# Batch 0's keys by block products, begun ahead of m, and a new order of the first loads

## The chip, the cores and the metric

The kernel runs on one core of one Trainium2 chip. The metric is the time of one execution on the device, in microseconds (us). Each version is run several times, and the median is compared. The engines are TensorE (PE), VectorE (DVE), ScalarE (ACT), GpSimd (POOL) and SyncE (SP, which issues most of the transfers).

## The reference

For each of 16 batches there are 100 tokens `x` of width 640 and 722 context rows of width 384, of which the last four (`ca`) are treated apart. All numbers are float32.

```python
query = hidden_states @ Wq
keyt = enc @ Wk                # enc: the first 718 context rows
valt = enc @ Wv
hs = _mha(query, keyt, valt)   # 8 heads of 80
ca_q1 = jnp.einsum('btc,th->bch', ca, Wq_ca)[:, indices, :]
ca_hs1 = _mha(ca_q1, residual, residual)
ca_hs2 = _mha(ca_hs1 @ Wq, ca @ Wk_ca, ca @ Wv_ca)
out = (hs + ca_hs2) @ Wout + b_out + residual
```

## The kernel before

**Tiling.** The context's 718 rows are cut into three thirds of 239 or 240 (`KT` = 240), each of which is two halves of up to `KN` = 120; the width 384 is three chunks of 128 (`CC` = 3), and 640 is five (`HC` = 5). The list `KC` numbers the six halves. `enc` holds the context of one batch, transposed, seven of its nine chunk-by-third pieces in one tile and two in a tile called `rest`.

**Two ways to the keys and values.** The plain way multiplies each third by each chunk of weights: `first_keys` with `chunk_keys` does so for batch 0's keys (line 565), nine products of 128x240 for each of five output chunks, and `first_values` for its values (line 381). The other way is a scheme of 15 block products in place of 18, in the manner of fast matrix multiplication: `enc_sums` (line 506, 13 additions on GpSimd) and `weight_sums` (line 528, 12 subtractions on VectorE) make sums of pieces; the classes `Values` and `Keys` then run products of these sums in the order of `V_PLAN` and `K_PLAN`. A block of keys is two matmuls of 128x240 (line 471). The first result for a place is copied there by ScalarE (line 413), and each later one is added by VectorE (line 411). The blocks use PSUM banks named A to E: `Keys.open` takes A and B from the pool psk, C to E from the pool ps1. `last_keys` does the fifth output chunk the plain way. From batch 1 on, keys and values come by blocks; the weight sums for that were made in the prologue.

**The second attention.** `m` (line 1036) is Wq transposed times the keys of the last four tokens for all batches, k2 (line 1013, masked by five VectorE multiplications at line 1025 into `k2T`). VectorE copies each chunk of m (line 1044), `keys()` spreads one batch's part of it into `m2` on GpSimd (line 718), and `Second.products` multiplies it by x (line 746). `scores1` is GpSimd work on what came out (lines 781 and 788), followed by a softmax.

**PSUM.** There are three pools of two slots: psk and ps1 of one bank, ps2 of two banks (`pair`, or `bank` for the first half of a pair). `psum()` takes turns between psk and ps1 by a counter, `turn`.

```python
    def psum(name):

        turn[0] += 1
        return (psumk if turn[0] % 2 else psum1)(name)
```

**Order of the work.** There are two regimes. The prologue, up to line 1123, is ordered by the planner of the framework, which may bring ready work forward on each engine; only loads marked `in_order` keep their order among themselves, and blocks under `tc.issue_after` stay behind a named instruction. From `tc.manual_schedule` (entered just before the loop over the 16 batches) each of the five engines runs its instructions in the order of the code. The prologue is, in the code's order: loads; five idle matmuls (line 1001); the first values for four of the six halves; k2 and m; the second attention's first steps for batch 0; 15 transposes of Wk (line 1059, copied into `wk_sb` at line 1062); 15 copies that lay Wq out as `wq_sb` (lines 1070 and 1077); the weight sums for Wk; batch 0's keys; the four tokens' values (line 1090); and the queries for batches 0 and 1 (line 541). The loop's first step then makes scores (line 620), in two slots of ps2 for the first and third pair of halves. The remaining two halves of batch 0's values are made in the loop.

**Loads.** The transfers issued by SP and ScalarE share eight completion semaphores in turn, and the instruction that issues a transfer waits until the one eight places earlier has landed. Wk, transposed, is loaded in nine pieces (`load_packed`, eight of them of 32 partitions) into the tile that later holds the keys; Wq transposed is loaded into the tile that later holds Wout.

Of the kernel before, what the change touches and what calls it, by code (L numbers as in the profile page):

```python
# [10 lines left out]
ALU = mybir.AluOpType  # L11
# [4 lines left out]
NH, D = 8, 80  # L16
# [116 lines left out]
def kernel(  # L133
# [134 lines left out]
    )  # L268
    enc = enc_tile("enc_0"), rest_tile("rest_0")

    def load_first(lo, hi, u, cols):

        for c in range(lo, hi):
            k = u * (KT - 1)
            in_order(
                nc.sync.dma_start(
                    out=a_raw(enc, u, c)[:, cols],
                    in_=enct[0][:, c, k + cols.start : k + cols.stop],
                )
            )  # L280

    load_first(0, CC, 1, slice(0, KN))
    for g in range(2):
        for c in range(CC):
            nc.scalar.dma_start(
                out=wv_sb[:, 2 * c + g],
                in_=wv[c * P : (c + 1) * P, g * (H // 2) : (g + 1) * (H // 2)],
            )
    load_first(0, CC, 1, slice(KN, KT))
    load_first(0, CC, 2, slice(0, KT))  # L290
    tokens = vb_tile("tokens")
    cat_sb = tokens[:, CC, : CC * B * T].rearrange("p (c n) -> p c n", c=CC)
    wkca_sb = tokens[:, :CC, :]
    in_order(nc.sync.dma_start(out=cat_sb, in_=cat.rearrange("p c b t -> p c (b t)")))
    in_order(nc.sync.dma_start(out=wkca_sb, in_=wkca.rearrange("(c p) n -> p c n", p=P)))
    wqt_sb = wout_sb
    wkt_sb = kT.rearrange("p c u k -> p c (u k)")
    in_order(nc.sync.dma_start(out=wqt_sb, in_=wqt.rearrange("(c p) r -> p c r", p=P)))
    load_first(0, CC, 0, slice(0, KT))
    xT = inp.tile([P, 2, HC, S], F32, tag="xT", name="xT_0")  # L300
    in_order(nc.sync.dma_start(out=xT, in_=xt[0:2].rearrange("b p c s -> p b c s")))
    ca_0 = small.tile([S, T, S], F32, tag="ca", name="ca_0", bufs=2)
    in_order(nc.sync.dma_start(out=ca_0, in_=cas[0].unsqueeze(0).to_broadcast([S, T, S])))
    load_packed(
        lambda **ends: in_order(nc.sync.dma_start(**ends)), wkt_sb[:, :, :CAD], wkt
    )
    halves = [t[:, u] for t in [scores_tile(f"wq_{i}") for i in range(NP)] for u in range(2)]
    room = halves.pop()
    wq_in = [t[:, :H] for t in halves]
# [224 lines left out]
            for tag, n in (("qp", 2), ("qz", 1))  # L534
        ]

    def queries(p, xT, tiles, n):
        qp, qz = tiles
        q_ps = psum(f"q_ps_{p}_{n}")
        for c in range(HC):  # L540
            nc.tensor.matmul(  # L541
                q_ps[:, : 2 * S].rearrange("p (j s) -> p j s", j=2),
                wq_sb[:, c, n * P : (n + 1) * P],
                xT[:, :, c, :],
                start=(c == 0),
                stop=(c == HC - 1),
            )
        if n < 4:
            nc.scalar.copy(qp[:, n // 2, n % 2], q_ps[:, : 2 * S])
        else:  # L550

            for u in range(2):
                nc.scalar.mul(
                    qz[:, 0, :, u * S : (u + 1) * S],
                    q_ps[:, : 2 * S].rearrange("p (j s) -> p j s", j=2),
                    qmask[:, u : u + 1],
                )


    def chunk_keys(n, banks, weights, enc):  # L560
# [18 lines left out]
                )  # L579
            )  # L580
        return copies

    def first_keys(enc):
        for n in range(HC - 1):
            banks = [psum(f"kT_ps_0_{n}_{k}") for k in range(2)]
            weights = [wk_sb[:, 2 * c + n % 2, n // 2] for c in range(CC)]
            chunk_keys(n, banks, weights, enc)
        last_keys(0, enc)

    def last_keys(b, enc):  # L590
        banks = pair(f"kT_ps_{b}")
# [409 lines left out]
        nc.tensor.matmul(idle_ps[:, :P], idle, idle, start=True, stop=True)  # L1001


    for i in (1, 4, 2, 5):
        first_values(i, enc, (act, act))
    weight_sums(nc.vector, wv_sb, there=wv_there)


    k2_ps = psum("k2_ps")
# [11 lines left out]
    for n, heads in enumerate(HEADS):  # L1021
        cols = len(heads) * B * T
        k2T.append(room[:, at : at + cols])
        at += cols
        nc.vector.tensor_tensor(
            k2T[n].rearrange("p (h k) -> p h k", h=len(heads)),
            k2_ps[:, n * B * T : (n + 1) * B * T]
            .unsqueeze(1)
            .to_broadcast([P, len(heads), B * T]),
            hmask[:, n, : len(heads)].unsqueeze(2).to_broadcast([P, len(heads), B * T]),  # L1030
            ALU.mult,
        )
    for c in range(HC):
        m_ps = psum(f"m_ps_{c}")
        for n, heads in enumerate(HEADS):
            nc.tensor.matmul(
                m_ps[:, heads[0] * B * T : (heads[-1] + 1) * B * T],
                wqt_sb[:, n, c * P : (c + 1) * P],
                k2T[n],
                start=(n == 0),  # L1040
                stop=(n == HC - 1),
                skip_group_check=True,
            )
        copied = nc.vector.tensor_copy(
            m_sb[c].rearrange("p (b h t) -> p h b t", h=NH, t=T),
            m_ps.rearrange("p (h b t) -> p h b t", h=NH, b=B),
        )
        nc.sync.dma_start(out=m_d[c], in_=m_sb[c])
    second = Second(0, xT, ca_0)
    keys(load_m(0))  # L1050
    summed = second.products()
    second.copy()
    second.scores1()
    keys(load_m(1))

    for c in range(HC):
        w_ps = psum(f"w_ps_{c}")
        for cc in range(CC):
            nc.tensor.transpose(
                w_ps[:, cc * P : (cc + 1) * P], wkt_sb[:, c, cc * P : (cc + 1) * P], ident  # L1060
            )
        act(
            wk_sb[:, c % 2 : 6 : 2, c // 2] if c < HC - 1 else wk4,
            w_ps[:, : CC * P].rearrange("p (a n) -> p a n", a=CC),
        )

    with tc.issue_after(summed.ins):
        for c in range(HC):
            for u in range(2):
                nc.vector.tensor_copy(  # L1070
                    wq_sb[:, c, 2 * u * P : 2 * (u + 1) * P].rearrange(
                        "p (a r k) -> p a r k", a=2, r=RG
                    ),
                    wq_in[c].rearrange("p (r k) -> p r k", r=RG)[:, :, u * D : u * D + 64]
                    .rearrange("p r (a k) -> p a r k", a=2),
                )
            nc.vector.tensor_copy(
                wq_sb[:, c, 4 * P :].rearrange("p (h k) -> p h k", h=NH),
                wq_in[c].rearrange("p (h k) -> p h k", h=NH)[:, :, 64:],
            )  # L1080
    with tc.issue_after(summed.ins):
        weight_sums(nc.vector, wk_sb, False)
    first_keys(enc)
    weight_sums(nc.vector, wk_sb, True)

    va = wide("va")[:, : H // 2]
    va_ps = psum("va_ps")
    for c in range(CC):
        for n in range(2):
            nc.tensor.matmul(  # L1090
# [8 lines left out]
    for n in range(2):  # L1099
# [1 line left out]
            out=va_d[:, n * (H // 2) : (n + 1) * (H // 2)],  # L1101
            in_=va[n * B * T : (n + 1) * B * T],
        )
    with tc.issue_after(copied.ins):
        nc.vector.tensor_reduce(
            qmask, ident.rearrange("p (r u k) -> p u r k", r=RG, u=2), AX.XY, ALU.add
        )
    tiles = queries_tiles(0)
    for n in range(HC):
        queries(0, xT, tiles, n)  # L1110

    xT_at = [None]
    last, enc_next, second_next = None, load_rest(1, load_enc(1)), Second(1, xT)
    engines = {
        mybir.EngineType.Pool,
        mybir.EngineType.PE,
        mybir.EngineType.DVE,
        mybir.EngineType.Activation,
        mybir.EngineType.SP,
    }  # L1120
    ctx.enter_context(tc.manual_schedule(engines=engines))
    for b in range(B):
        p = b // 2
        e_in, now = enc, second
# [271 lines left out]
```

## Time and profile before

| what | value |
|---|---|
| median of 3 runs | 944.52 us (944.06 to 944.62) |
| the profiled execution: its time, its span | 944.18 us, 942.5 us |
| granted clock of TensorE, mean | 1.0 |
| busy: PE, DVE, ACT, POOL | 934.5, 675.5, 364.6, 623.1 us |
| chain that ended last, share of PE | 94% |
| values of batch 0, four halves: first product to end | 3.66 to 18.28 us |
| keys of batch 0 on PE | 30.94 to 49.33 us |
| first scores on PE | 59.68 us |

Times in the profile count from the span's start. Busy times overlap, so they do not add up to the span. A row of the order in time gives start, duration, engine, line, operation, output and inputs, the shape, how many instructions are merged in it, and in brackets how long the engine was idle before it and what ended that. One float32 product shows as two matmul records.

### The profile page before, as it was taken

How to read it: one execution, taken by the hardware profiler on the slowest of the kernel's cores; microseconds unless marked ns; L12 is line 12 of the kernel's file. 1: busy time of each engine (PE TensorE's matmuls, PEld its weight loads, DVE VectorE, ACT ScalarE, POOL GpSimd, SP SyncE). 2: the span in 40 equal slices, each digit the busy share in tenths (PEclk: the TensorE clock that was granted, in tenths of full speed). 3: DMA queues.
4: the chain of work that ended last, by engine and by line, in shares of the span. 5: the costliest groups of instructions: out<-in, count | busy, mean ns of one | idle time of the engine just before them, and what ended most of it. 6: DMA issues, size and time to landing. Idle time of an engine off the chain costs nothing.

```text
span 942.5 us, 25630 instructions
## 1 busy us (share of the span) xinstructions
PE 934.5 (99%) x11215; PEld 796.0 (84%) x11215; DVE 675.5 (72%) x1084; ACT 364.6 (39%) x605; POOL 623.1 (66%) x565
## 2 busy tenths in 40 slices
PE   9999999999999999999999999999999999999998
PEld 6998879788797888988789887987989888897866
DVE  3559794977929788595955959578693886949684
ACT  1244443424334244433424334244431534334241
POOL 5857966776738767595863948757694576848514
PEclk9999999999999999999999999999999999999999
DMA  8822024040310404004050120403113030110300
GB/s 263 297 64 84 3 70 127 1 130 3 94 60 1 117 2 130 10 9 123 1 151 3 35 83 1 139 1 95 38 40 113 1 112 7 54 58 1 95 8 29
DMA packets 45367, 62.48 MB, mean 66 GB/s; under 512 B 13448, under 2 KB 37320, under 8 KB 43656
## 3 DMA queue, kind: packets, MB, share of 16 engines
q1 hardware_dynamic: 41720, 42.97, 15.1%
q0 software_dynamic: 2512, 16.72, 6.0%
q8 instruction: 88, 1.44, 0.7%
q10 hardware_dynamic: 1024, 1.15, 0.4%
q14 instruction: 23, 0.19, 0.1%
HBM read 55.26 MB, written 5.57 MB: 65 GB/s over the span
## 4 chain that ended last, share of the span: by engine, by line
PE 94%; DVE 3%; issue 1%; DMA 0%; ACT 0%; POOL 0%; ACTq 0%; DVEq 0%
PE s_ps L620 12%; PE a_ps L1317 12%; PE v_psA L440 10%; PE v_psB L440 8%; PE kT_ps L565 8%; PE q_ps L541 7%; PE k_psA L471 7%; PE o_ps L951 7%; PE k_psB L471 6%; PE v_psC L440 3%; PE k_psC L471 3%; PE y_ps L746 2%; PE v_psD L440 2%; PE v_psE L440 2%; PE v_ps L381 1%; PE k_psE L471 1%
## 5 line engine op out<-in xcount | busy, mean ns | idle before, releaser
L781 POOL TENSOR_TENSOR e<-ca,g 100x800 f32<-100x800 f32 x64 | 99.3, 1563 | 142.5 <-DVE most L1156 127.5
L870 POOL TENSOR_TENSOR hs<-vb,p 100x640 f32<-100x640 f32 x64 | 105.6, 1659 | 46.1 <-DVE p L856 32.3
L877 POOL TENSOR_TENSOR hs<-hs,hs 100x640 f32<-100x640 f32 x48 | 113.9, 2372 | 3.8
L1317 PEld LDWEIGHTS a_ps<-vs,st 120*36 120x36 f32 (+3 forms) x3072 | 109.1, 125 | 5.6 <-issue 5.5
L1317 PE MATMUL a_ps<-vs,st 120*36 120x81 f32 (+3 forms) x3072 | 111.9, 233 | 0.0
L506 POOL TENSOR_TENSOR enc<-enc 128x240 f32<-128x240 f32 x135 | 98.8, 741 | 16.7 <-DMA enc<-in_enct 9.6
L440 PE MATMUL v_psA<-wv_sb,enc 128*120 128x320 f32 x352 | 109.7, 434 | 0.0
L1144 DVE TENSOR_TENSOR st<-st,over 120x1600 f32<-120x1600 f32 x48 | 107.5, 2242 | 0.0
L637 ACT COPY st<-s_ps 120x800 f32<-120x800 f32 x64 | 49.7, 829 | 135.6 <-PE s_ps L620 135.6
L620 PE MATMUL s_ps<-qp,kT 32*120 32x100 f32 x3072 | 97.6, 263 | 0.0
L620 PEld LDWEIGHTS s_ps<-qp,kT 32*120 32x120 f32 x3072 | 94.8, 179 | 1.6 <-issue 0.2
L788 POOL TENSOR_TENSOR e<-e,e 100x800 f32<-100x800 f32 x48 | 90.4, 1884 | 3.8
L440 PE MATMUL v_psB<-wv_sb,enc 128*120 128x320 f32 x296 | 91.8, 433 | 0.0
L471 PE MATMUL k_psA<-enc,wk_sb 128*128 128x240 f32 x360 | 87.7, 366 | 0.2 <-DVE kT L411 0.2
L1329 DVE RECIPROCAL rs<-a_ps 100x4 f32<-100x4 f32 x32 | 5.8, 183 | 111.0 <-PE a_ps L1317 111.0
L471 PEld LDWEIGHTS k_psA<-enc,wk_sb 128*128 128x128 f32 x360 | 68.2, 190 | 17.3 <-POOL e L788 0.7
L440 PEld LDWEIGHTS v_psA<-wv_sb,enc 128*120 128x120 f32 x352 | 63.0, 183 | 22.9 <-DVE vs L411 0.8
L1152 ACT ACTIVATE st<-st 120x1600 f32<-120x1600 f32 x48 | 73.9, 1539 | 21.8 <-DVE st L1144 21.7
L1156 DVE TENSOR_TENSOR most<-most,st 120x800 f32<-120x800 f32 x64 | 65.8, 1029 | 22.9 <-ACT st L631 21.8
L471 PE MATMUL k_psB<-enc,wk_sb 128*128 128x240 f32 x300 | 73.1, 366 | 0.0
L440 PEld LDWEIGHTS v_psB<-wv_sb,enc 128*120 128x120 f32 x296 | 54.1, 183 | 21.9 <-DVE vs L411 0.4
L541 PE MATMUL q_ps<-xT,wq_sb 128*128 128x200 f32 x400 | 69.1, 333 | 0.0
(146 smaller groups left out, 1734.1 us busy)
## 6 DMA issues: line engine op xcount, KB each, us to landing
vb<-va_d POOLq DMA_DIRECT2D x16, 1000.0 KB, 7.6
enc<-in_enct SPq DMA_DIRECT2D x30, 240.0 KB, 3.8
enc<-in_enct SPq DMA_DIRECT2D x15, 360.0 KB, 3.5
xT<-in_xt SPq DMA_DIRECT2D x8, 500.0 KB, 4.7
rest<-in_enct SPq DMA_DIRECT2D x31, 120.0 KB, 6.6
xn<-in_x SPq DMA_DIRECT2D x11, 320.0 KB, 4.1
out<-xn SPq DMA_DIRECT2D x11, 320.0 KB, 2.8
ca<-in_cas SPq DMA_DIRECT2D x16, 156.2 KB
```

Of the source, the lines that this page charges most:

```text
L440: nc.tensor.matmul(at[0][j][:KN, : H // 2], a_form(self.enc, f)[:, j * KN : (j + 1) * KN], wv_there.get(f, wv_sb[:, W_AT[f]]), start=first ...
L471: nc.tensor.matmul(at[:, i * KT : (i + 1) * KT], wk_sb[:, W_AT[f], i], a_form(self.enc, f), start=(first and i == 0), stop=last, skip_grou ...
L506: nc.gpsimd.tensor_tensor(out, left, right, op)
L541: nc.tensor.matmul(q_ps[:, : 2 * S].rearrange("p (j s) -> p j s", j=2), wq_sb[:, c, n * P : (n + 1) * P], xT[:, :, c, :], start=(c == 0), ...
L565: nc.tensor.matmul(bank[:, i * KT : (i + 1) * KT], weights[c], a_raw(enc, u, c), start=(i == 0 and c == 0), stop=(c == CC - 1), skip_group ...
L620: nc.tensor.matmul(s_ps[r][:n, 256 * a + lo : 256 * a + hi], kT[rows, c, u, j * KN : (j + 1) * KN], rhs, start=(a == 0 and c == 0), stop=( ...
L781: first = nc.gpsimd.tensor_tensor(to, self.ca[:, t, :].unsqueeze(1).to_broadcast([S, NH, S]), g[:, :, t].unsqueeze(2).to_broadcast([S, NH, ...
L788: nc.gpsimd.tensor_tensor(e, e, to, ALU.add)
L870: first = nc.gpsimd.tensor_tensor(to, vb[:S, t, :].rearrange("p (h d) -> p h d", h=NH), p2[:, :, t].unsqueeze(2).to_broadcast([S, NH, D]), ...
L877: nc.gpsimd.tensor_tensor(sums, sums, to, ALU.add)
L1144: return nc.vector.tensor_tensor(st[i], st[i], top.over[:KN].unsqueeze(1).to_broadcast([KN, 2, ROWS]), ALU.subtract,)
L1317: nc.tensor.matmul(a_v[lo:hi, h % 4], st[i // 2][: KEYS[i], i % 2, h * S + lo : h * S + hi], block(i, h // 4)[: KEYS[i], h % 4], start=(i ...
```

## The change

**Loads.** The first loads of the context's thirds take two chunks in one transfer where they lie side by side: two transfers for three. The first half of Wv's columns still comes in three transfers, the second half in one. The remaining third of the context is loaded right behind the other two, then Wk, then the four tokens with their key weights, and Wq transposed; x and `ca` come after that.

**Order by hand from the first values on.** `tc.manual_schedule` is entered before the first values instead of before the loop, so each engine runs the whole prologue in the code's order, which is rewritten: the first values, `enc_sums` for batch 0, the sums of Wv, the transposes of Wk, the sums of Wk, k2, five key blocks, m, the copies of Wq, two blocks, the second attention's first steps, the four tokens' values, and the queries with two blocks after each of the first four and `last_keys` before the fifth.

**Keys.** `first_keys` is gone; batch 0's keys are `Keys(0, enc)` and `last_keys(0, enc)`.

**Banks.** m takes its banks from ps1 alone; the four tokens' values and the queries of batches 0 and 1 take theirs from ps2 (`bank`).

```diff
+        k = u * (KT - 1)
+        for to, lo, hi in (
+            ((enc[0][:, :3], 0, 3),),
+            ((enc[1][:, :1], 0, 1), (enc[0][:, 3:5], 1, 3)),
+            ((enc[0][:, 5:7], 0, 2), (enc[1][:, 1:], 2, 3)),
+        )[u]:
             in_order(
                 nc.sync.dma_start(
...
-    load_first(0, CC, 1, slice(0, KN))
-    for g in range(2):
-        for c in range(CC):
+    load_first(1, slice(0, KN))
+    for g, parts in ((0, [slice(c, c + 1) for c in range(CC)]), (1, [slice(0, CC)])):
+        for c in parts:
             nc.scalar.dma_start(
...
-    load_first(0, CC, 1, slice(KN, KT))
-    load_first(0, CC, 2, slice(0, KT))
+    load_first(1, slice(KN, KT))
+    load_first(2, slice(0, KT))
+    load_first(0, slice(0, KT))
+    wkt_sb = kT.rearrange("p c u k -> p c (u k)")
+    load_packed(
+        lambda **ends: in_order(nc.sync.dma_start(**ends)), wkt_sb[:, :, :CAD], wkt
+    )
...
-    load_first(0, CC, 0, slice(0, KT))
...
-    load_packed(
-        lambda **ends: in_order(nc.sync.dma_start(**ends)), wkt_sb[:, :, :CAD], wkt
-    )
...
-    def queries(p, xT, tiles, n):
+    def queries(p, xT, tiles, n, get=psum):
         qp, qz = tiles
-        q_ps = psum(f"q_ps_{p}_{n}")
+        q_ps = get(f"q_ps_{p}_{n}")
...
+    ctx.enter_context(tc.manual_schedule(engines=engines))
     for i in (1, 4, 2, 5):
         first_values(i, enc, (act, act))
+    enc_sums(enc)
     weight_sums(nc.vector, wv_sb, there=wv_there)
+
+    for c in range(HC):
+        w_ps = psum(f"w_ps_{c}")
+        for cc in range(CC):
+            nc.tensor.transpose(
+                w_ps[:, cc * P : (cc + 1) * P], wkt_sb[:, c, cc * P : (cc + 1) * P], ident
+            )
+        act(
+            wk_sb[:, c % 2 : 6 : 2, c // 2] if c < HC - 1 else wk4,
+            w_ps[:, : CC * P].rearrange("p (a n) -> p a n", a=CC),
+        )
+    weight_sums(nc.vector, wk_sb)
...
+    k0 = Keys(0, enc)
+    k0.go(3)
+    k0.go(2)
     for c in range(HC):
-        m_ps = psum(f"m_ps_{c}")
+        m_ps = psum1(f"m_ps_{c}")
...
     keys(load_m(0))
-    summed = second.products()
+
+    for c in range(HC):
+        for u in range(2):
+            nc.vector.tensor_copy(
+                wq_sb[:, c, 2 * u * P : 2 * (u + 1) * P].rearrange(
...
+    k0.go(2)
+    second.products()
     second.copy()
     second.scores1()
     keys(load_m(1))
...
-    first_keys(enc)
-    weight_sums(nc.vector, wk_sb, True)
+    nc.vector.tensor_reduce(
+        qmask, ident.rearrange("p (r u k) -> p u r k", r=RG, u=2), AX.XY, ALU.add
+    )
 
     va = wide("va")[:, : H // 2]
-    va_ps = psum("va_ps")
+    va_ps = bank("va_ps")
...
+    xT_at = [None]
+    last, enc_next, second_next = None, load_rest(1, load_enc(1)), Second(1, xT)
     tiles = queries_tiles(0)
     for n in range(HC):
-        queries(0, xT, tiles, n)
...
+        queries(0, xT, tiles, n, bank)
+        k0.go(2)
+        if n == HC - 2:
+            last_keys(0, enc)
```

## The prediction

> **What bounds the kernel now.** I read three views: the page's shares, the order of TensorE's instructions over the first 75 us (the change touches nothing later), and the order of the other engines beside it. TensorE is busy for 934.5 of 942.5 us, so a microsecond less on it counts only if it then has the next operand at hand.
>
> ```profile
> PE 934.5 (99%) x11215; PEld 796.0 (84%) x11215; DVE 675.5 (72%) x1084; ACT 364.6 (39%) x605; POOL 623.1 (66%) x565
> ```
>
> TensorE's order in the prologue (start, duration, line, operation, count, idle before and what ended it):
>
> ```profile
> 6.01 0.80 PE L381 MATMUL v_ps<-wv_sb,enc 128*120 128x320 f32 x2 [0.68 <-DMA wv_sb<-in_wv]
> 6.64 0.71 PE L381 MATMUL v_ps<-wv_sb,rest 128*120 128x320 f32 x2
> 7.20 1.46 PE L381 MATMUL v_ps<-wv_sb,enc 128*120 128x320 f32 x4
> ...
> 9.03 1.24 PE L381 MATMUL v_ps<-wv_sb,enc 128*120 128x320 f32 x4
> ...
> 18.28 1.97 PE L1013 MATMUL k_ps<-tokens 128*64 128x64 f32 x60
> 20.76 6.86 PE L1036 MATMUL m_ps<-wq,wout_sb 128*128 128x128 f32 x50 [0.51 <-issue]
> ...
> 29.02 0.41 PE L746 MATMUL y_ps<-m,xT 128*100 128x96 f32 x2 [0.40 <-POOL m L718]
> 29.27 1.83 PE L1059 MATMUL w_ps<-ident,kT 128*128 128x128 f32 x13
> 30.94 1.38 PE L565 MATMUL kT_ps<-enc,wk_sb 128*128 128x240 f32 x6
> ...
> 51.02 8.72 PE L541 MATMUL q_ps<-xT,wq_sb 128*128 128x200 f32 x50
> 59.68 1.10 PE L620 MATMUL s_ps<-qp,kT 32*120 32x100 f32 x32
> ```
>
> Each product is two records. From 8.5 us on only 0.9 us is idle up to the scores at 59.68: the old prologue, which the planner filled, is nearly dense. VectorE, GpSimd and ScalarE beside it:
>
> ```profile
> 20.36 1.22 DVE L1025 TENSOR_TENSOR wq<-k_ps,hmask 128x128 f32<-128x128 f32 x5 [9.32 <-PE k_ps L1013]
> ...
> 27.65 0.69 DVE L1044 COPY m<-m_ps 128x512 f32<-128x512 f32 x1 [0.63 <-PE m_ps L1036]
> ...
> 32.34 2.43 DVE L528 TENSOR_TENSOR wk_sb<-wk_sb 128x256 f32<-128x256 f32 x7
> ...
> 29.52 5.41 POOL L718 TENSOR_TENSOR m<-m,hmask 128x64 f32<-128x64 f32 x1 [0.24 <-PE y_ps L746]
> ...
> 30.23 1.33 ACT L1062 COPY wk_sb<-w_ps 128x384 f32<-128x384 f32 x3
> ...
> 59.79 0.75 ACT L553 ACTIVATE qz<-q_ps,qmask 128x200 f32<-128x200 f32 x2 [1.37 <-PE q_ps L541]
> ```
>
> **Step 1, products saved: -2.43 us.** The old keys are 45 products of 128x240 in 18.23 us (30.94 or rather 31.10, where the chain of waits puts them, to 49.33), 0.405 us each. The new ones are 15 block products of two matmuls (30) and the 9 of last_keys: 39. Six fewer, 6 x 0.405 = 2.43. In the loop the same block products run at the same spacing (k_psA from 68.74, 0.20 us a record). This is all that TensorE gains; the other steps are waits.
>
> **Step 2, the second half of Wv as one transfer: +0.9.** Before, this half came as three transfers; TensorE used its first third at 6.64, and waited only for the last: the x4 row took 1.46 instead of 1.24, so its last product began at 7.86. The transfers moved 272, 268 and 231 GB/s in the slices 2 to 4, 4 to 6 and 6 to 8 us, its engines 82 to 97% busy: the bytes ahead of the last third are the same now, so I put the landing of the whole at 7.75 too. All three products of the half then start there: 7.75 + 3 x 0.54 = 9.4, against 8.49 before. Bounds: -0.3 (fewer issues, 0.4 us each on the queue, let it land early enough) and +1.3. The larger first transfer for two thirds of the tokens costs nothing: TensorE waited until 6.01 for Wv there anyway; uncovered, it would be some tenths. So the values end, which I call T0, at 18.28 + 0.9 = 19.2.
>
> Is Wk there at T0? Ahead of it and with it stand 1080 KB of thirds, 960 KB of Wv and 960 KB of Wk, 3.07 MB. The old slices had moved that by 13 us; with Wk alone at the 139 to 202 GB/s of the slices 20 to 24, when it loaded, it is there by 15.5 to 17.5. The tokens' keys (1.08 MB at some 400 GB/s) follow by 18 to 20, needed at 21.2; Wq transposed (1.64 MB) by 22 to 24, needed near 30. I price this step at nothing, with 2 us of cover; behind it the queue of SP holds only x, ca and Wq, which land by some 31 at the latest and are used after 37.
>
> **Step 3, the keys' start: +2.86.** From T0 TensorE does 15 transposes (1.97) and k2 (1.90, 18.35 to 20.25), then block A7 and block B13. B13 opens the second bank of the psk pool. That pool has two: A has one, and the other was given to k2_ps, since the counter `turn` is odd there (1 idle, 8 values, 5 transposes, k2 is the 15th). So B13 cannot begin before the five multiplications of L1025 have read k2_ps; and VectorE now has the twelve sums of Wk ahead of them in its queue. Their chain from T0: the fourth copy of transposed Wk on ScalarE 2.30 (0.54 for the last copy of values, four copies at some 0.43 as in the 1.33-for-three row); sums 11 x 0.337 + 0.42 = 4.13 (2.43 for seven); GpSimd is then at its new thirteen sums of thirds (from 13.4, 0.70 each, to 22.6), so VectorE waits for half of one, 0.35; L1025 1.22; hand-over 0.05. Together 8.05. TensorE has 1.97 + 1.90 + 0.81 = 4.68 to do before: it waits 3.37 (some 0.55 before A7, for its weight sum, the rest before B13). The 0.51 before m is gone, since L1025 is done by then: +2.86. Bounds: B13 needn't wait for that bank, then only the 0.55 stays, +0.04; or VectorE waits for all the sums that GpSimd has left at 21.5, 1.1, then +3.6. Behind the waiting B13 all of TensorE's queue stands.
>
> **Step 4, a stall before y: +1.1.** After m, TensorE has A9 and E6 (1.62) and four products of y (0.8). The fifth needs GpSimd's last multiplication of L718, which needs the last copy of m (0.2 + 0.69 after m). Right behind that copy VectorE now has the 15 copies of Wq (29.65 to 32.43 before, 2.78). The row at 29.52 shows what they do to GpSimd: the same multiplication took 5.41 us instead of 0.29, to the end of 22 VectorE instructions that ran without a gap. So it is done at 0.9 + 2.78 + 0.3 = 3.98 after m, while TensorE is ready at 2.42: a wait of 1.5, less the old 0.40. Bounds: -0.4 (GpSimd gets in at once) and +1.3.
>
> The Trainium skill ("SBUF — State Buffer", "Who interferes with whom") says that the two engines take turns by instruction: whoever starts first holds the shared ports for the whole instruction. By that the multiplication would enter behind one copy and this step would be -0.4; the 5.41 us row, with 22 instructions in one hold, speaks against it, and I go by the row.
>
> **Step 5, the scores' banks: +0.85.** The queries now use banks of the two-slot pool ps2. The first scores take two slots, and the second was the last query's. Its two qz copies end 0.86 us after the query's product (59.68 to 60.54); before, the scores began at 59.68 beside them. Bounds: 0 and +0.95.
>
> **Hidden.** The nine new additions into the keys on VectorE (0.67 each) come when it is otherwise idle, between products spaced by queries of 1.73. The multiplications for batch 1 move behind scores1 on GpSimd and hold back the `rest` load for batch 1 (its room is m's) until about 56; the sums of thirds then end near 70 instead of 68.05, and are first needed by batch 1's keys at 72, so nothing, with 1 to 2 us of cover for the ones used first. The first softmax ends near 64, needed at 66.
>
> **Sum.** -2.43 + 0.9 + 2.86 + 1.1 + 0.85 = **+3.28**. The profiled execution took 944.18 (span 942.5): 947.5. It lies 0.3 below the median shown, 944.52. Own range 946 to 949.
>
> **Rivals.** *Within 0.2% (0.2):* step 3 takes its lower end because the keys get a bank that k2 does not hold: 947.5 - 2.8 = 944.6. For it: slots are given out by the planner, which I only see through the counter. Against: two slots leave no third. *Faster (0.13):* the planner, not the code, still orders the section. Before, it put y's last product among the transposes, out of code order (28.24 to 29.02). Then steps 3 and 4 are filled with ready work and end at -0.51 and -0.4, step 5 at 0: -2.43 + 0.9 - 0.91 = -2.4, 941.7. It decides when over 5.2 us of the 5.7 priced in steps 3 to 5 are filled. Against: the loop, under the statement that now stands earlier, runs as written. *Slower still (0.12):* the idle time before B13 costs TensorE its clock. The first products ran at half the later rate (128x128 records 0.21 us apart at 1.7 to 3.2), and no gap after 3.7 us exceeded 0.92, so the trace can't exclude it; twice the time for some 3.4 us, as at the start, adds 1.7: 949.2, and with late loads 951.
>
> The Trainium skill ("TensorE: Matmul & The Clock Gate", "What's actually happening") puts the loss of clock at an idle window of about 3.4 us; by that, an estimate, the 2.8 before B13 would just escape. No row here shows it.
>
> **Numbers.** Forecast 0.55. The range takes the first rival whole and reaches from 943.2 to 949.5; left out are most of the faster case and half of the slowest. 0.2% (1.9 us) is about what a measurement here can tell from no change. Faster 0.13; same 0.20; slower 0.67.
>
> **What would show it.** Step 1: 60 records on L471 for batch 0, 18 on L565. Step 2: idle time before the products of the second half, ended by Wv. Step 3: some 2.8 us before the first k_psB, with L1025 ending it. Step 4: 1.5 before the last y, ended by L718, whose row is some 3 us long. Step 5: 0.8 early in the first scores, ended by L553. The scores then start at 62 to 63. If the gap before k_psB is under 1 us, the forecast is wrong.

## The result and the profile after

The changed kernel takes **951.53 us** (median of 4 runs, 950.68 to 951.79) against 944.57 (944.06 to 944.86): ratio 1.007 [1.0058, 1.0081]. It is some 7 us slower. The prediction had the direction, 947.5, but the time lies above its range, which ended at 949.5. The profiled execution took 951.79, its span is 950.1 (before: 944.18 and 942.5), so the two traces differ by 7.6.

First the page, busy times and instructions of each engine.

```profile
PE 936.6 (99%) x11203; PEld 796.6 (84%) x11203; DVE 676.7 (71%) x1093; ACT 364.2 (38%) x603; POOL 626.1 (66%) x578
```

There are 12 matmul records less, as six saved products should give, and yet TensorE is busy for 2.1 us more. A busy time that grows while the work shrinks means that matmuls ran slower. TensorE's order in time of the changed kernel shows where (start, duration, line, operation, count, idle before and what ended it):

```profile
7.45 1.13 PE L387 MATMUL v_ps<-wv_sb,enc 128*120 128x320 f32 x2 [2.02 <-DMA wv_sb<-in_wv]
8.97 1.42 PE L387 MATMUL v_ps<-wv_sb,rest 128*120 128x320 f32 x2 [0.38 <-DMA wv_sb<-in_wv]
...
20.92 0.70 PE L387 MATMUL v_ps<-wv_sb,rest 128*120 128x320 f32 x2
21.46 1.80 PE L1019 MATMUL w_ps<-ident,kT 128*128 128x128 f32 x15
23.19 1.97 PE L1033 MATMUL k_ps<-tokens 128*64 128x64 f32 x60
26.65 1.05 PE L477 MATMUL k_psA<-enc,wk_sb 128*128 128x240 f32 x4 [1.49 <-DVE wk_sb L534]
30.25 1.94 PE L477 MATMUL k_psB<-enc,wk_sb 128*128 128x240 f32 x4 [2.54 <-DVE wq L1045]
31.98 1.81 PE L477 MATMUL k_psD<-enc,wk_sb 128*128 128x240 f32 x4
33.58 1.72 PE L477 MATMUL k_psA<-enc,wk_sb 128*128 128x240 f32 x4
35.14 0.97 PE L477 MATMUL k_psB<-enc,wk_sb 128*128 128x240 f32 x4
35.95 6.76 PE L1059 MATMUL m_ps<-wq,wout_sb 128*128 128x128 f32 x50
...
65.77 0.45 PE L619 MATMUL s_ps<-qp,kT 32*120 32x100 f32 x4
66.67 0.98 PE L619 MATMUL s_ps<-qp,kT 32*120 32x100 f32 x26 [0.45 <-ACT qz L559]
```

Read it from the top. The last third of Wv's *first* half comes 1.4 us later than before (7.45 against 6.01), so the values end at 21.46, not 18.28. The first key block waits 1.49 us for the weight sums, the second 2.54 us for L1045, which empties the bank of k2. Of the four blocks behind that wait, three take 1.56 to 1.73 us to the next one's start; the fourth takes 0.81, as all of them should. The scores stop for 0.45 us for the qz copies.

Why three blocks take twice the time is seen in busy time by stretches (columns: length, then busy time and count of PE, of its weight loads PEld, of DVE, ACT and POOL, then the granted clock, DMA share and GB/s). The stretches are cut where the granted clock of the changed kernel could change: in the trace's clock records it does so only at 4.37, 7.79, 11.20, 28.27 and 35.09, all whole multiples of 3.413 us apart.

```profile
4.37:7.79 3.42, 1.40 (x5) 0.57 (x4) 0.00 (x0) 0.00 (x0) 2.38 (x5) 1.00 0.96 282
7.79:11.20 3.41, 3.03 (x6) 1.44 (x5) 2.14 (x5) 0.43 (x1) 2.25 (x6) 0.50 1.07 242
24.86:28.27 3.41, 1.35 (x15) 0.84 (x10) 3.34 (x10) 0.53 (x1) 0.23 (x1) 1.00 1.04 302
28.27:31.68 3.41, 1.44 (x4) 1.28 (x5) 1.83 (x8) 0.03 (x1) 0.00 (x0) 0.50 1.01 390
```

Twice a window in which TensorE was busy for only 1.35 to 1.40 us is followed by one at half clock. The second loss lasts two windows, to 35.09, since the window from 28.27 to 31.68 was again mostly idle.

The budget between the two traces, each row with the forecast beside it:

| part | forecast, us | traces, us |
|---|---|---|
| step 1: six products fewer | -2.43 | -2.43 |
| step 2: values end | +0.9 | +3.18 (waits +1.73; half clock from 7.79, some +1.5 by what the rest leaves; the first product 0.1 earlier) |
| step 3: waits before the keys, 1.49 + 2.54 - 0.51 | +2.86 | +3.52 |
| half clock in blocks 2 to 4 (1.73 + 1.60 + 1.56 - 3 x 0.81) | rival only | +2.46 |
| step 4: y | +1.1 | -0.40 |
| step 5 and a pause in the scores: first score to z, 8.42 - 7.34 | +0.85 | +1.08 |
| what is left (z to the end +0.43, the rest -0.24) | | +0.2 |
| sum | +3.28 | +7.6 |

### The profile page after: what moved, and what is told of

The parts are those of the page before. It is cut to its first block, busy times and chain, and to the rows that moved or that the text cites. A ratio compares the mean times of both kernels' runs of the same rounds, so it can differ in the third digit from the quotient of the medians.

```text
span 950.1 us, 25625 instructions
## 1 busy us (share of the span) xinstructions
PE 936.6 (99%) x11203; PEld 796.6 (84%) x11203; DVE 676.7 (71%) x1093; ACT 364.2 (38%) x603; POOL 626.1 (66%) x578
## 3 DMA queue, kind: packets, MB, share of 16 engines
HBM read 55.26 MB, written 5.57 MB: 64 GB/s over the span
## 4 chain that ended last, share of the span: by engine, by line
PE 95%; DVE 3%; DMA 1%; ACT 0%; issue 0%; ACTq 0%; DVEq 0%
PE s_ps L619 12%; PE a_ps L1319 12%; PE v_psA L446 10%; PE v_psB L446 9%; PE k_psA L477 8%; PE q_ps L547 7%; PE o_ps L950 7%; PE k_psB L477 7%; PE kT_ps L571 6%; PE v_psC L446 3%; PE k_psC L477 3%; PE y_ps L745 2%; PE v_psE L446 2%; PE v_psD L446 2%; PE k_psD L477 1%; PE v_ps L387 1%
## 5 line engine op out<-in xcount | busy, mean ns | idle before, releaser
L512 POOL TENSOR_TENSOR enc<-enc 128x240 f32<-128x240 f32 x144 | 105.2, 740 | 7.5
L477 PE MATMUL k_psA<-enc,wk_sb 128*128 128x240 f32 x384 | 94.4, 369 | 1.7 <-DVE wk_sb L534 1.5
L477 PEld LDWEIGHTS k_psA<-enc,wk_sb 128*128 128x128 f32 x384 | 73.2, 192 | 19.3 <-issue 1.6
L477 PE MATMUL k_psB<-enc,wk_sb 128*128 128x240 f32 x320 | 78.9, 370 | 2.6 <-DVE wq L1045 2.5
L477 PEld LDWEIGHTS k_psB<-enc,wk_sb 128*128 128x128 f32 x320 | 61.2, 192 | 13.2 <-issue 3.3
```

The source lines that it names most:

```text
L477: nc.tensor.matmul(at[:, i * KT : (i + 1) * KT], wk_sb[:, W_AT[f], i], a_form(self.enc, f), start=(first and i == 0), stop=last, skip_grou ...
L512: nc.gpsimd.tensor_tensor(out, left, right, op)
```

## The experiments

The theory was: the wait for k2's bank and the clock that it costs are the larger half, the merged first loads the rest. Its rivals: that the clock is not lost through the wait, or that the loads are late for their order and not their size. Each median is of 5 to 12 executions; the kernel before had medians of 944.24 to 944.45 beside them. Kernels with the changed kernel's loads place the values' end between 19.9 and 22.4 in their traces, so a difference under 1 us between two single experiments is not used without the trace.

**The bank of k2.** k2 takes its place from ps2, and `turn` stays as it was for what follows.

```diff
-    k2_ps = psum("k2_ps")
+    turn[0] += 1
+    k2_ps = bank("k2_ps")
```

> The changed kernel, with k2 in a bank of the pool ps2 instead of psk (the counter is moved on by one, so that all later banks stay as they are). Theory 'bank': the 2.54 us before the first k_psB are a wait for k2's bank, and the half clock from 28.27 to 35.09 us follows from that idle time. Then the gap before the first k_psB is gone, the 1.49 before k_psA stays (a weight sum ends it), the 12 products after it run at 0.20 us a record, m starts at 26.65 + 5 x 0.81 = 30.7 instead of 35.95, and the time falls by about 5.2, to 946.3. Rival 'weights': VectorE's twelve sums are late anyway and k_psB waits for its own sum; then the gap stays at over 2 us, and the time at 951.

Measured: 945.96 (945.36 to 948.18), ratio 1.002 [1.0011, 1.0028]: 5.6 us of the 7. TensorE's order of this kernel:

```profile
26.54 1.51 PE L477 MATMUL k_psA<-enc,wk_sb 128*128 128x240 f32 x4 [2.53 <-DVE wk_sb L534]
27.84 1.81 PE L477 MATMUL k_psB<-enc,wk_sb 128*128 128x240 f32 x4
```

The wait before the second block is gone. The one before the first is longer than in the changed kernel (2.53 for 1.49), since the values ended earlier in this trace, at 20.30, and the weight sums did not come earlier. The profiled execution was the longest of eleven (948.18): here the one wait left still cost the clock, from 26.98 to 30.39. So the bank is shown to be the largest single cause; how much of the 5.6 is the wait itself and how much the clock, the next run shows.

**The clock alone.** Six idle products fill the wait before the first block and eleven that before the second; the bank is left as it was.

```diff
-    k0.go(3)
+    warm_ps = bank("warm_ps")
+    for _ in range(6):
+        nc.tensor.matmul(warm_ps[:, :P], idle, idle, start=True, stop=True)
+    k0.go(1)
+    for _ in range(11):
+        nc.tensor.matmul(warm_ps[:, :P], idle, idle, start=True, stop=True)
+    k0.go(2)
```

> The changed kernel, with idle products of 128x128 on TensorE, whose result nobody reads: 6 before the first key block (1.3 us) and 11 between the first and the second (2.3 us). The waits for VectorE stay as they are; only the idle time is filled. Theory 'clock': k_psB still starts at about 30.25, but the granted clock stays 1.0 from 24 to 36 us, the three blocks that took 0.92, 0.79 and 0.75 us longer take 0.81 each, m starts at 33.5, and the time falls by 2.4, to 949.1. Rival 'operands': the blocks are slow because of what they read (weights just summed, thirds just summed); then they stay slow, and the time at 951.5.

Measured: 948.77 (948.08 to 949.73), 1.0047 [1.0034, 1.006]. Its TensorE:

```profile
27.25 2.62 PE L1059 MATMUL warm_ps<-idle 128*128 128x128 f32 x22
29.71 1.03 PE L477 MATMUL k_psB<-enc,wk_sb 128*128 128x240 f32 x4
30.58 0.97 PE L477 MATMUL k_psD<-enc,wk_sb 128*128 128x240 f32 x4
31.39 0.97 PE L477 MATMUL k_psA<-enc,wk_sb 128*128 128x240 f32 x4
```

The second block still begins late, at 29.71 for 30.25 (the sums of Wk took 4.86 for 5.33 us), but the blocks follow each other by 0.81 to 0.87, and no half clock shows after 11.62. From the second block's start to m it is 3.30 us for 5.70, so 2.4 us in the traces are the clock. Work that nobody reads made the kernel 2.8 us faster. The wait's price was thus some 2.5 us of idle time and nearly as much again of clock.

**The loads, all single.** The new order is kept, but the thirds and Wv's second half come in single pieces as before.

```diff
-            ((enc[1][:, :1], 0, 1), (enc[0][:, 3:5], 1, 3)),
-            ((enc[0][:, 5:7], 0, 2), (enc[1][:, 1:], 2, 3)),
+            ((enc[1][:, :1], 0, 1), (enc[0][:, 3:4], 1, 2), (enc[0][:, 4:5], 2, 3)),
+            ((enc[0][:, 5:6], 0, 1), (enc[0][:, 6:7], 1, 2), (enc[1][:, 1:], 2, 3)),
...
-    for g, parts in ((0, [slice(c, c + 1) for c in range(CC)]), (1, [slice(0, CC)])):
+    for g, parts in ((0, [slice(c, c + 1) for c in range(CC)]), (1, [slice(c, c + 1) for c in range(CC)])):
```

> The changed kernel, with its first loads in single pieces as before (three transfers each for the thirds u=1 and u=2, and for the second half of Wv); the new order of the loads stays. Theory 'pieces': the start was lost to the larger transfers. The values end at 18.3 to 18.5 instead of 21.46, the half clock from 7.8 to 11.2 us is gone, and the time falls by 3.0, to 948.5. Rival 'order': what comes after the first pieces (the third u=0 and Wk, issued from 4.6 us on, where nothing of the kind was on the queue before 8.8) takes the transfer engines' time from Wv; then the values still end after 20, and the time stays over 950.

Measured: 948.88 (947.4 to 949.37), 1.0042 [1.0029, 1.0056], 2.65 less than the changed kernel. The values end at 18.44, 0.16 from before. The new *order* of the loads is therefore not the cause; the merging is. The earlier start doesn't all arrive at the end, since the first block now waits 2.04 for the sums. Transfers in the fifth microsecond (last number: GB/s), in before, the changed kernel and this one:

```profile
4.00:5.00 1.00, 1.00 (x4) 0.52 (x3) 0.49 (x1) 0.42 (x1) 1.00 (x3) 1.00 0.91 269
```
```profile
4.00:5.00 1.00, 1.00 (x4) 0.31 (x3) 0.00 (x0) 0.01 (x1) 1.00 (x3) 1.00 0.84 159
```
```profile
4.00:5.00 1.00, 1.00 (x3) 0.58 (x3) 0.00 (x0) 0.48 (x1) 1.00 (x3) 1.00 0.80 242
```

The changed kernel moved 110 KB less than before in that microsecond, two thirds of one piece of Wv (128 x 320 numbers, 164 KB), and a piece of Wv is what TensorE waited for. But the rate differs from execution to execution: the six traces with the changed kernel's loads moved 147 to 212 GB/s there, the three with single pieces 189 to 242, the three with before's loads 208 to 269. What does not overlap is when TensorE uses the last third of Wv's first half: at 6.76 to 7.45 in those six, at 6.16 to 6.61 with single pieces, and at 6.01 to 6.38 with before's loads.

**One half of the merging at a time.** Thirds single (the first two lines of the diff above), then Wv's second half single (its last line).

> The changed kernel, with the thirds u=1 and u=2 in single pieces as before and the second half of Wv still in one transfer. If what counts is how early SP can issue the later loads (eight completion semaphores are shared in turn, and fewer transfers free them sooner), this does nearly all that single pieces throughout do: the last third of Wv's first half lands near 6.0 instead of 7.4, the second half near 7.8, the values end near 19.3, 949.4. If the large transfer of Wv is what slows the start, it does nothing: 951.5.

> The changed kernel with only the second half of Wv in single pieces; the thirds stay in the larger transfers. The thirds in single pieces alone gave 949.7, both 948.9. If the two are separate, this gives some 0.8 less than 951.5, 950.7: the second half's first piece is there when the first half's products end, but Wv's last third of the first half still lands near 7.4, since SP issues u=2 from 3.5 us on as before. If this alone restores the start (values end by 18.6), the large transfer of Wv was the cause and not the early issue: 948.9.

Measured: 949.7 (948.22 to 950.12), 1.0053 [1.004, 1.0065], and 949.4 (948.53 to 950.37), 1.0048 [1.0035, 1.0061]. In the traces Wv's last third is used at 6.61 and 6.50, against 7.45 in the changed kernel and 6.46 with all single. Either edit brings that piece nearly back, so neither half is the sole cause, and their gains (1.83 and 2.13, against 2.65 for both) don't add up. Values end at 20.72 (the first, at half clock until 10.62) and 19.28. In the fifth microsecond they moved 166 and 214 GB/s: the first has its piece early at a rate as low as the changed kernel's. So the low rate is not the whole cause either. That the merging delays the piece is shown; by what means is open. It is not told by whether SP issues transfers meanwhile: SP did so in the kernel with the idle products, which moved 212, and not between 4.4 and 5.8 in the kernel with both repairs (below), which moved 190.

**Both repairs**, the bank and the single loads:

> The changed kernel with both edits that helped: k2 in a bank of ps2, and the first loads in single pieces. If the two losses are separate, they add: 951.5 less 5.6 (k2's bank alone) less 2.7 (single pieces alone) is 943.3, just below the kernel before. What stays is a wait of some 2 us before the first k_psA (weight sums), with or without half a clock for 3.4 us after it (1.7 us), so single runs may differ by that much. Rival: an earlier start only moves the work up against the next load or against GpSimd's sums of thirds, and the wait before k_psA grows by what was gained: 945 to 946.

Measured: 943.66 (942.92 to 945.21), 0.9993 [0.9984, 1.0001]. The two repairs together take off 7.87. Its first block still waits 2.20 us for the weight sums, yet the clock stays. Stretches of this kernel, cut at its own clock borders, and the one of the first experiment (the bank alone) that lost the clock:

```profile
20.01:23.43 3.42, 2.01 (x61) 1.86 (x60) 2.97 (x4) 0.78 (x3) 3.26 (x5) 1.00 1.03 392
23.43:26.84 3.41, 2.46 (x12) 2.35 (x13) 3.37 (x10) 1.12 (x2) 0.53 (x1) 1.00 1.05 326
```
```profile
23.57:26.98 3.41, 0.88 (x18) 0.75 (x13) 3.34 (x6) 0.00 (x0) 2.00 (x3) 1.00 1.05 310
```

Here the wait (22.18 to 24.38) lies across a border, and each window is busy for 2.0 us or more; there the wait of 2.53 lay within one window, busy for 0.88. The borders stand elsewhere in every execution, so the same wait costs its clock by chance. That would explain why the times of kernels with such a wait spread by 2 to 3 us; it was seen only in the profiled executions. A rival stands beside it: the first full clock came anywhere from 4.2 to 13.4 us in the fourteen traces, so the start can spread the times too.

**The stall that didn't come.** One small VectorE instruction that doesn't involve GpSimd's data, the qmask reduction, is put between the last copy of m and the copies of Wq, to see whether what stands right behind decides.

```diff
     keys(load_m(0))
+    nc.vector.tensor_reduce(
+        qmask, ident.rearrange("p (r u k) -> p u r k", r=RG, u=2), AX.XY, ALU.add
+    )
...
     keys(load_m(1))
-    nc.vector.tensor_reduce(
-        qmask, ident.rearrange("p (r u k) -> p u r k", r=RG, u=2), AX.XY, ALU.add
-    )
```

> The changed kernel, with the short VectorE reduction that makes qmask moved from behind the copies of Wq to just before them. In the kernel before, GpSimd's multiplication at 29.52 began 0.13 us before the first of a row of VectorE copies, right behind a reduction, and took 5.41 us; in the changed kernel it began 0.16 us after the first copy and took 0.29. This edit puts it again between a reduction and the first copy. Theory 'who comes first': it is held until the row of 15 copies ends, 2.8 us, the last product with x waits some 1.5 us, and the time is 953. Rival 'turns': it enters between two copies as in the changed kernel, 0.3 us, and the time stays at 951.5.

Measured: 950.82 (950.28 to 951.45), 1.007 [1.0058, 1.0083], the same as the changed kernel within the noise of the start. GpSimd's last multiplication took 0.293 us in it and 0.294 in the changed kernel, whose rows are (VectorE, then GpSimd):

```profile
42.75 0.69 DVE L1067 COPY m<-m_ps 128x512 f32<-128x512 f32 x1 [0.63 <-PE m_ps L1059]
43.36 0.60 DVE L1077 COPY wq_sb<-wq 128x256 f32<-128x256 f32 x2
```
```profile
43.52 0.29 POOL L717 TENSOR_TENSOR m<-m,hmask 128x64 f32<-128x64 f32 x1 [0.97 <-DVE m L1067]
```

GpSimd starts among VectorE's first two copies and loses nothing; these take 0.60 where later pairs take 0.48, so VectorE paid 0.12. There is no hold in either kernel, so the added instruction decided nothing.

**m first, in before's order of loads.** Another arrangement by hand: k2 and m come ahead of the transposes of Wk, as before; the sums of Wk, `last_keys`, the second attention's steps, the copies of Wq and the tokens' values follow, and then seven key blocks and the queries, with two blocks after each.

```diff
-    k0 = Keys(0, enc)
-    k0.go(3)
-    k0.go(2)
     for c in range(HC):
-        m_ps = psum1(f"m_ps_{c}")
+        m_ps = psum(f"m_ps_{c}")
...
+    weight_sums(nc.vector, wk_sb)
+    last_keys(0, enc)
+    second.products()
+    second.copy()
+    second.scores1()
+    keys(load_m(1))
...
+    k0 = Keys(0, enc)
+    k0.go(3)
+    k0.go(2)
+    k0.go(2)
...
-        queries(0, xT, tiles, n, bank)
+        queries(0, xT, tiles, n, bank if n < HC - 1 else psum1)
```

> The block products for batch 0's keys, in another order, with the loads exactly as in the kernel before: values, k2 with its five multiplications, m (in all four single banks), the transposes of Wk, last_keys, the first products with x, the four tokens' values, then seven blocks and the queries with the other eight between them; on VectorE the sums of Wk come behind the copies of m, and the copies of Wq behind the sums. TensorE then has 3.65 + 1.0 + 1.8 us of work that needs no weight sum while VectorE makes the sums. Theory 'waits': the block products are worth their 2.43 us once nothing waits; the old waits before the products with x (0.4) go too and no clock is lost: scores at 57 instead of 59.68, 941.8. Rival: the sums of Wk meet GpSimd's sums of thirds or the copies of Wq come too late for the queries, and the blocks wait as before: 944 or more.

Measured: 943.69 (943.24 to 948.9), 1.0004 [0.9991, 1.0017]; a miss by 1.9. Two of its eleven executions took over 948; no trace shows why. TensorE starts the scores at 58.24, 1.4 earlier than before, and loses it again there: it stands twice with nothing to wait for that the profile names, which the profile calls "issue". Below, one of the two, and GpSimd's row of the same kernel beside 15 copies and one reduction of VectorE (35.37 to 38.3):

```profile
63.49 0.77 PE L613 MATMUL s_ps<-qp,kT 32*120 32x100 f32 x18 [0.99 <-issue]
```
```profile
35.53 4.01 POOL L774 TENSOR_TENSOR e<-ca,g 100x800 f32<-100x800 f32 x1 [6.57 <-DVE g L748]
```

This instruction takes 1.53 elsewhere in the kernel; here, 4.01. So the hold that the prediction feared exists (as in before's 5.41 row), with the very copies of Wq, but not where it was feared.

**The scores: bank and late loads.** Three runs: the last query in ps1, so that the scores find a free pair; the second batch's keys part ahead of `scores1`, so that the loads of `rest` and what is queued behind it are issued at 48 to 53 us instead of 61 to 64; and both with the two repairs.

```diff
-        queries(0, xT, tiles, n, bank)
+        queries(0, xT, tiles, n, bank if n < HC - 1 else psum1)
```
```diff
-    second.scores1()
     keys(load_m(1))
+    second.scores1()
```

> The changed kernel, with the fifth query product of batches 0 and 1 in a bank of ps1 instead of ps2. Theory 'bank': the scores' second pair of banks no longer waits for the two qz copies; the gap of 0.45 us early in the scores goes, and with it some 0.35 later in them: 951.5 less 0.8, 950.7. Rival: the scores then wait elsewhere (their first pair, or the third pair of halves, whose banks ScalarE frees), and the time stays at 951.5.

> The changed kernel, with one thing undone: GpSimd's multiplications for batch 1 ahead of scores1, as the planner had put them. The loads of `rest`, Wout and x are issued near 50 instead of 61 to 64 us and land before the scores begin at 65.8. If the pause of 0.3 us at 70.6 in the scores came from these loads, it goes: 951.2; if it did not, 951.5. It costs nothing elsewhere unless scores1 (1.5 us later) then holds up the first softmax and z_ps: that would be some tenths more.

> The changed kernel with every loss so far taken out at once: k2 in ps2, first loads in single pieces, the last query in ps1, and GpSimd's multiplications for batch 1 put back ahead of scores1 (they hold the room of `rest`; in the changed kernel the loads of `rest`, Wout and x behind it on SP moved from 38 to 42 us to 61 to 64, into the scores, whose instructions are many and short). Theory 'all waits': 943.7 (k2's bank and single pieces) less 0.8 (qz) less up to 0.4 (pauses in the scores): 942.5, of which some 2 us are still the wait before the first k_psA. Rival: the scores lose the time elsewhere, 943.7.

Measured: 951.29 (950.23 to 951.79), 1.0073 [1.0061, 1.0086]; 950.26 (949.38 to 950.82), 1.0058 [1.0046, 1.007]; and **942.12** (941.87 to 944.43), **0.9978 [0.997, 0.9987]**. The first is the changed kernel's time within its range, and the second is 1.3 less, of which its trace has 0.25 in the scores and the rest in no one place. The time from the first score to z:

| scores to z, us | loads issued late, as in the changed kernel | loads issued early |
|---|---|---|
| last query in ps2 | 8.42 (changed kernel); 8.17 to 8.82 in the eight traces of this kind | 8.17 |
| last query in ps1 | 8.43 | 7.34 (both, with the repairs) |

Before it was 7.34. The bank's wait thus costs 0.83 (8.17 against 7.34). The free bank alone gained nothing: the 0.45 is gone, and a pause of 0.75 appears, ended by nothing that the profile names:

```profile
70.08 0.76 PE L619 MATMUL s_ps<-qp,kT 32*120 32x100 f32 x17 [0.75 <-issue]
```

Where the loads come early too, neither is left. TensorE's order of the last kernel:

```profile
25.45 1.05 PE L477 MATMUL k_psA<-enc,wk_sb 128*128 128x240 f32 x4 [1.37 <-DVE wk_sb L534]
26.33 0.97 PE L477 MATMUL k_psB<-enc,wk_sb 128*128 128x240 f32 x4
...
59.39 1.10 PE L619 MATMUL s_ps<-qp,kT 32*120 32x100 f32 x32
...
66.73 0.75 PE L807 MATMUL z_ps<-y,e 100*32 100x33 f32 x64
```

This version is faster than both kernels. Its profiled execution was the longest of eleven, 944.43, with half clock until 10.33; eight of the eleven lie between 941.87 and 942.32.

**m first, without the late loads.** The same for the other arrangement, with the products of the second attention ahead of `last_keys`.

```diff
-    last_keys(0, enc)
     second.products()
     second.copy()
-    second.scores1()
+    last_keys(0, enc)
     keys(load_m(1))
+    second.scores1()
```

> The order with m ahead of the keys and the old loads, with two repairs: the first products with x before last_keys (0.77 us was lost before last_keys, waiting for ScalarE's copy of its weights), and GpSimd's multiplications for batch 1 ahead of scores1. In the run without them TensorE stood still 0.99 us in the scores and 1.01 before the products of z with nothing in the profile to wait for, while some 200 to 370 GB/s of loads ran that the kernel before had at 38 to 42 us. Theory 'loads in the scores': these two gaps go, and the time is 943.7 less 0.8 less up to 1.5: 941.5 to 942. Rival: the two gaps are the instruction stream's own, wherever the loads are; then 943.0.

Measured: 943.74 (942.84 to 947.54), 0.9997 [0.9988, 1.0006], a miss. The pause in the scores is gone (z at 65.76, 1.1 earlier), though 302 GB/s moved beside them from 62 to 64. One of 0.58 now stands within z, while nothing is being loaded (0 GB/s from 65 to 67):

```profile
66.73 0.56 PE L801 MATMUL z_ps<-y,e 100*4 100x33 f32 x42 [0.58 <-issue]
```

So a load at the moment of the pause is neither enough nor needed. The traces show what goes with the pauses. The six in the scores and z of 0.4 us or more that end by nothing named, in five kernels, stand at two places of TensorE's stream: counted from the trace's start in records of products and weight loads, before the 961st instruction or before the 1217th. These are 256 apart. Each ended 1.2 to 1.6 us after a packet of 16 KB on the page's queue for instructions (q8) had landed, which is 64 bytes for each of 256. What differs is when that packet starts. In the three kernels whose loads come early, the one before the 961st starts after 687 to 694 instructions, with nothing else in transfer in the 3 us before, and the 961st follows without a gap. In nine with late loads, it starts after 818 to 892, with 331 to 397 GB/s in transfer in those 3 us, and in all nine the 961st starts 0.19 to 1.25 us after the one before it, the longest where the packet started latest. The kernel with the idle products has late loads too, but its packet starts before they do, after 664; it has no gap, and from the first score to z it too took 8.17. All this fits a TensorE that waits for its own instructions while other loads hold these up. No run changed the instructions' loading alone, so it is read from the traces and not shown by experiment.

## Why the prediction was wrong

The repairs add up: from 951.53 the bank takes off 5.57 (945.96), the single loads 2.30 (943.66), the free bank for the scores with the early loads 1.54 (942.12). What is left under before, 2.3, is about what step 1 promised, in part by chance: this kernel's trace still waits 1.37 before the first block, where before's waits of 0.51 and 0.40 are gone. The forecast lay 4.3 us under the traces' difference of 7.6: step 2 makes 2.3 of them, the clock 2.5, step 3 0.7 and step 5 with what is left 0.4, less 1.5 for the stall of step 4 that didn't come.

- **Step 1** was right in its count: six products less, 18 records on the old line of the fifth chunk. Its -2.43 could be seen in the time only when everything else was repaired.
- **Step 2 was mis-sized**, +3.18 instead of +0.9. The step that failed is "the bytes ahead of the last third are the same now, so I put the landing of the whole at 7.75 too". TensorE waited for that half until 8.97. The bytes were the same, the rate in this trace was not (159 instead of 269 GB/s between 4 and 5 us, though that isn't all). Wv's *first* half, which the change leaves alone, came late already, and the step looked only at the half that it merges. The wait then emptied a clock window: some 1.5 more.
- **Step 3 was right in its mechanism and nearly in its size**: the bank of k2, released by L1045 behind the sums (shown by the bank's experiment). The waits were 1.49 and 2.54 for 0.55 and 2.8. The sums ran 5.33 us for 12, not 4.13 + 0.35:

```profile
23.65 5.33 DVE L534 TENSOR_TENSOR wk_sb<-wk_sb 128x256 f32<-128x256 f32 x12 [9.23 <-ACT wk_sb L1022]
```

  The first two took 0.9 each beside GpSimd's sums of thirds, which ran from 15.78 to 25.1 (priced: 13.4 to 22.6), where I had priced half of one. Across the traces the row takes 4.36 where it begins as those end (the last query in ps1, from 24.61) and 6.27 to 6.39 where it begins 3 to 4 us ahead of that; the first block then waits 0.53 or 2.0 to 2.6. That would be why values that end earlier gained little there; no run moved GpSimd's sums.
- **What the wait costs beside itself was put into a rival.** "Slower still: the idle time before B13 costs TensorE its clock" got 0.12 and +1.7. It came, +2.46 in the trace, and the idle products removed it: shown. That rival's text came to 951 with late loads, near the result, but by luck: step 2's upper bound, +1.3 for +0.9, makes 949.2 only 949.6, and a second loss of the clock, at the start, stood nowhere. The range ended at 949.5. Step 3 itself forecast a wait of 2.8 us, and a trace with no gap over 0.92 after 3.7 us could not say what such a one costs; both ends of that belonged in the range.
- The Trainium skill ("TensorE: Matmul & The Clock Gate", "What's actually happening") has the window right: about 3.4 us and free-running; the clock records here change at multiples of 3.413 us. But the step from "an idle window" to "a wait of 2.8 us escapes" failed: over all traces, the ten windows with 0.85 to 1.51 us of work in 3.41 lost the clock, and those with 1.82 or more kept it (1.82 with the bank alone, from 6.50; 1.89 with Wv's second half single, from 21.09). Between 1.51 and 1.82 no window was seen.
- **Step 4 failed**: no stall, -0.40 instead of +1.1. I went by the 5.41 row, and the rule of the skill that speaks against it ("SBUF — State Buffer", "Who interferes with whom": whoever starts first has the ports for one instruction) fits what happened here and in the reduction's experiment (0.29 us for GpSimd, 0.12 lost by VectorE). Yet GpSimd was held for 4.01 us beside the same copies when they stood at another place. What decides between turns and a hold is open; one row shows that a hold can be, not that it will be.
- **Step 5** was right about the wait (0.45, ended by L559), the bank and the size (0.83 in the two traces without a pause); alone, its removal gained nothing, since TensorE then came to the pause sooner.
- **Hidden** was half wrong: the `rest` load held back by GpSimd was put at nothing, and the text had it until "about 56"; it was issued at 61.1, and with x and Wout it ran beside the scores at 278 GB/s (64 to 68 us) and 330 (68 to 72), where before at most 12 ran. With the free bank this cost 1.1 (8.43 against 7.34); that TensorE's instructions came late by it is read from the traces.
- The rival "the planner still orders" is out: all rows stand in the code's order. "Within 0.2%" rested on k2 not holding the keys' bank; it did.

## What to carry to other kernels

Ask of each wait that a new order makes not only how long it is, but how much work is left in the 3.4 us around it: where less than half was left here (1.51 us or less), the next window ran at half clock, and the wait cost about twice. When an order is written by hand, follow each PSUM slot to the instruction that frees it, and that instruction to what stands before it in its engine's queue: giving one tile another pool was worth 5.6 us here. Merging first loads can delay a piece that is not itself merged: here it cost 2.3 to 2.65 us, though the first half of Wv stayed in single pieces.

## What was not expected of the hardware

- Half clock after windows that were not idle: up to 1.51 us of work in 3.41 was too little, 1.82 enough. A window at half clock was followed by another with up to 2.33 us of work in it, and by full clock with 3.03 or more. Six and eleven idle products (the eleven: 22 records in 2.6 us) held the clock.
- The first loads moved 147 to 212 GB/s in the fifth microsecond in six traces of the same loads, so one trace's rate says little.
- TensorE stood 0.40 to 1.01 us in the scores and z with nothing that the profile could name, always before its 961st or 1217th instruction, and went on 1.2 to 1.6 us after 16 KB of instructions had landed. Four of the six pauses had under 10 GB/s of loads beside them; what they have in common is that this packet had started late.
- GpSimd beside a row of VectorE copies: 0.294 us, or held for 4.01 instead of 1.53.
